# Linear attention on one core: where FP4 weight pieces are unpacked, and in which order the sums around the G products are formed

## The chip, the cores and the metric

The kernel runs on one core of a Trainium2 chip. The metric is the device time of one execution in microseconds (us); a kernel's time is the median of its runs. Less is better. Engine names in this text: PE multiplies matrices, PEld loads its weights, DVE is the vector engine, ACT the activation engine, POOL the general engine, SP issues most DMAs.

## The reference, cut to what matters

Two layers run one after the other on x of 2 x 1024 x 512 (float32), each an attention and an FFN with a residual and a layernorm behind each. Only the first attention and the preparation of the first FFN's weights are touched here:

```
q = elu(x Wq^T) + 1;  k = elu(x Wk^T) + 1;  v = x Wv^T          # 16 heads of 32
kv = k^T v  per head;  z = 1 / (q . sum_t k + 1e-6)
out = (q kv) z;   x = layernorm(x + out Wo^T)
w_gu, w_down = FP4 tables * scales                              # weights of the next FFN
```

The rest (the FFN with these weights, a gated linear attention with chunks of 64, an FFN over the 512 best rows) is computed by code that the change leaves alone.

## The kernel before, in words

The 2048 rows are four blocks of 512 (blk 0 to 3); two blocks make a batch b. The loop `for b in range(B)` (L629 on, in the function `body`) goes through a batch's first attention in the order **k of the first block, k of the second, q of the first, q of the second**. For b = 0 the first k (of block 0) is computed plainly ahead of the loop, so the four passes of seven products that the loop calls k are, in time: k of block 1, then (b = 1) k of blocks 2 and 3; the q passes are those of blocks 0 to 3. "The first k" of the change's title is that of block 1, "the fourth k" that of block 3.

**Seven products instead of eight.** A 512x512 by 512x512 product is cut into a 2x2 of 256-wide parts and done with Winograd's seven products. The price is sums of parts on DVE: S1 = A21 + A22, S2 = S1 - A11, S3 = A11 - A21, S4 = A12 - S2 of the left factor, T1 = B12 - B11, T2 = B22 - T1, T3 = B22 - B12, T4 = B21 - T2 of the right one. `by_seven` (L338) does so for q and k; it is a generator that yields after each of its first products, and `run` (L588) puts a list of other steps into each pause. Its lines in the profile: S1 L356, S2 L357, S3 L358, copies and sums of the results L363 to L384, elu in L304, L305 (ACT) and L306 (DVE).

**From v to G.** `add_xk` (L393, matmuls L400) sums x^T k over a batch. `values` (L452) makes the small per-head matrices from it, `G_rows` (L465) multiplies them with Wo: 32 small matmuls (L473), four ACT copies into G (L477), then the sums T1, T2, T4, T3 of G (`sums_of_weights`, L335, in the order traced). So x + out Wo^T becomes x + q G, with q already weighted by z (`weigh`, L441 to L447).

**The q G products.** `o_products(blk)` (L494) is a generator as well, for blocks 0, 1 and 2; block 3 goes through `add_o` (L542) with whole products. It first forms S1 (L515), S2 (L516) and A21 - A11 in place of A21 (L517), then runs seven products (matmuls at L507); behind each product DVE adds the PSUM bank to x (L513). Products 1, 3, 5 and 7 add up in **one** PSUM bank, grow: product 3 may begin only when L513 has read the sum of product 1, product 7 when L513 has read that of product 5, and product 3 needs S2 and T2. Products 4 and 6 share the bank P7 (side) in the same way, and need A21, T3 and T4. Product 7 needs S4 (L524).

**FP4 pieces.** 27 jobs of `unpack` (L244) turn packed weights into floating point: a DMA of the piece (L248, SP), two passes on DVE (L251, L252), one ACT pass (L254). Pieces of wgu are 128 x 704 (16 of them), then pieces of wdn 128 x 512 (11). Two buffers (`pk`, bufs=2) hold them. The steps `job(n)` in `run` put n jobs into a pause; `unpack_some` ties a job's instructions behind the last elu (L306) that is traced by then.

**What sets the order.** PE's order is written by hand: `behind()` makes each matmul follow the one traced before it. On the other engines the program builder picks, among the instructions that are ready by its own estimate, the one traced first; an engine then works its queue strictly in that order. A tile that takes the place of another of the same tag waits until the last reader of the old one is done. The rooms for G's sums and for S1 are staged[2] in batch 0; in batch 1 they are a tile TG in the place of Wo (tag A3).

Of the kernel before, what the change touches and what calls it, by code (L numbers as in the profile page):

```python
# [10 lines left out]
F32 = mybir.dt.float32  # L11
# [10 lines left out]
P = 128  # L22
# [51 lines left out]
def body(ctx: ExitStack, tc: tile.TileContext, a: dict, out: bass.AP):  # L74
    nc = tc.nc
# [20 lines left out]
    def acc_bank(name):  # L96
        return bank("acc", name)
# [5 lines left out]
    staged = [  # L103
        wfp4.tile([P, to - at, C], F32, tag=f"wdn{i}", name=f"staged{i}")
        for i, (at, to) in enumerate(zip(wdn_parts, wdn_parts[1:]))
    ]
# [20 lines left out]
    def place_w(i, name):  # L127
        return wpool.tile([P, KC, C], F32, tag=f"A{i}", name=name)
# [27 lines left out]
    t, src = new_xT(0)  # L156
# [84 lines left out]
    wk = s1.enter_context(tc.tile_pool(name="s1", bufs=2))  # L241
# [85 lines left out]

    pieces_of = lambda t: t.rearrange("p (k c) -> p k c", k=2)

    def sums_of_weights(w, rooms):  # L330

        B11, B12, B21, B22 = (w[:, 2 * e : 2 * e + 2, 256 * o : 256 * o + 256] for e in range(2) for o in range(2))
        T1, T2, T4, T3 = (*rooms, B12)[:4]
        for dst, x, y in ((T1, B12, B11), (T2, B22, T1), (T4, B21, T2), (T3, B22, B12)):
            nc.vector.tensor_sub(dst, x, y)  # L335
        return T1, T2, T3, T4

    def by_seven(x, w, T, rooms, pairs, ready):  # L338
# [3 lines left out]
        T1, T2, T3, T4 = T  # L342
        S1, S2, S3 = rooms

# [11 lines left out]
        nc.vector.tensor_add(S1, A21, A22)  # L356
        nc.vector.tensor_sub(S2, S1, A11)  # L357
        nc.vector.tensor_sub(S3, A11, A21)  # L358
# [9 lines left out]
        yield  # L368
        product(grow, S2, T2, False)
        nc.scalar.copy(c21, p)  # L370
        side = mm_bank("P7")
        p7 = product(side, S3, T3, True)
        nc.vector.tensor_sub(S2, A12, S2)
        yield
# [4 lines left out]
        yield  # L379
        product(grow, S2, B22, False)  # L380
        elu1(c12, p)
# [8 lines left out]
    pairs_of, mv_of, G_of, acc_of, ksum_of = {}, {}, {}, {}, {}  # L390
# [59 lines left out]
    vkm_of, qT, TG, o_of, parts = {}, {}, {}, {}, []  # L450

    def values(b):  # L452
# [9 lines left out]

        nc.scalar.copy(vkm_of[b], vk.rearrange("p (c d) -> p c d", c=KC))

    def G_rows(b):  # L465


        gp = [acc_bank("gp") for _ in range(4)]
        quad = lambda i: slice(32 * i, 32 * i + 32)
        for j in range(4):  # L470
            for c in range(KC):
                with behind():
                    last_pe[0] = nc.tensor.matmul(  # L473
                        gp[j][quad(c)], vkm_of[b][quad(j), c, quad(j)], Wo[quad(j), c], start=True, stop=True
                    ).ins
        for c in range(KC):
            nc.scalar.copy(G_of[b][:, c], gp[c])  # L477

        room = staged[2] if b == 0 else place_w(3, "TG")
        rooms = slices(room, 0, 3)  # L480
        if b:

            rooms.append(pieces_of(wk.tile([P, 512], F32, tag="qT3", name="T3", bufs=1)))
        TG[b] = sums_of_weights(G_of[b], rooms), pieces_of(room[:, 3])

    def turned(blk, i):
        if i == 0:
# [6 lines left out]
    def o_products(blk):  # L494

        A11, A12, A21, A22 = (qT[blk][:, 2 * e : 2 * e + 2, 256 * t : 256 * t + 256] for t in range(2) for e in range(2))
        G = G_of[blk // 2]
        B11, _, B21, B22 = (G[:, 2 * e : 2 * e + 2, 256 * o : 256 * o + 256] for e in range(2) for o in range(2))
        (T1, T2, T3, T4), S1 = TG[blk // 2]
        S2 = pieces_of(wk.tile([P, 512], F32, tag="qS", name="qS", bufs=1))  # L500

        def product(ps, a, b, first, t, o):

            with behind():
                for r in range(2):
                    for k in range(2):
                        ins = nc.tensor.matmul(  # L507
                            ps[:, 256 * r : 256 * r + 256], a[:, k, r * P : (r + 1) * P], b[:, k],
                            start=first and r == 0 and k == 0, stop=k == 1, skip_group_check=True,
                        ).ins  # L510
            last_pe[0] = ins
            x = x_t[blk][:, 2 * t : 2 * t + 2, 256 * o : 256 * o + 256]
            nc.vector.tensor_add(x, x, ps.rearrange("p (r c) -> p r c", r=2))  # L513

        nc.vector.tensor_add(S1, A21, A22)  # L515
        nc.vector.tensor_sub(S2, S1, A11)  # L516
        nc.vector.tensor_sub(A21, A11, A21)  # L517
        grow = acc_bank("grow")
        product(grow, A11, B11, True, 0, 0)
        yield  # L520
        product(acc_bank("P2"), A12, B21, True, 0, 0)
        yield
        product(grow, S2, T2, False, 1, 0)
        nc.vector.tensor_sub(A12, A12, S2)  # L524
        yield
        side = acc_bank("P7")
        product(side, A21, T3, True, 1, 1)
        yield
        product(grow, S1, T1, False, 1, 1)
        yield  # L530
        product(side, A22, T4, False, 1, 0)
        yield
        product(grow, A12, B22, False, 0, 1)
        yield
        mv = mv_of[blk] = sp.tile([P, 4, 2], F32, tag="mv", name="mv")
        with tc.issue_after(weighed[0]):
            for i in range(4):
                row_stats(mv[:, i], x_t[blk][:, i])
            layernorm(x_t[blk], mv, by=nc.gpsimd)
        yield  # L540
# [57 lines left out]
    def some_xk(blk, *part):  # L598
        return [lambda i=i: add_xk(blk, i) for i in part]

    def turns(blk, *part):
        return [lambda i=i: turned(blk, i) for i in part]

    def some_o(blk, n):

        def one():
            if blk not in o_of:
                o_of[blk] = o_products(blk)
            next(o_of[blk])

        return [one] * n
# [4 lines left out]
    job = lambda n: [lambda: unpack_some(n)]  # L616
# [7 lines left out]
    step = lambda f, *x: [lambda: f(*x)]  # L624
# [4 lines left out]
    for b in range(B):  # L629
        i, j = 2 * b, 2 * b + 1  # L630
        if b:
            run(
                k_products(i),
                turns(1, 0, 1) + job(1), job(1),
                turns(1, 2, 3) + some_o(1, 1) + job(1), some_o(1, 2) + job(1), some_o(1, 5) + job(1),
            )
        q_ready = [] if b else step(q_weights)
        run(
            k_products(j), [],
            some_xk(i, 0, 1) + job(2), some_xk(i, 2) + job(1) + q_ready, some_xk(i, 3) + job(1), job(1 + b),  # L640
        )
        if b == 0:
            Ts["q"] = sums_of_weights(Wq, slices(staged[0], 0, 3))
        else:

            Tq = place_w(1, "Tq")
            for n in range(3):
                nc.scalar.copy(Tq[:, n], staged[0][:, n])
            Ts["q"] = (*slices(Tq, 0, 2), Ts["q"][2], *slices(Tq, 2, 3))
            S_rooms[0] = pieces_of(Tq[:, 3])  # L650
        run(
            q_products(i, lambda t: weigh(i, t)), [],
            some_xk(j, 0, 1) + job(1 + b), some_xk(j, 2) + step(spread_ksum, b) + job(1), some_xk(j, 3) + job(1 + b),
        )
        if b == 0:
            xT[2] = load_xT(2)
        split = [step(split_some, n) if b else [] for n in range(4)]
        rings["free"] = (rings["sum"][(turn_of["sum"] + 1) % 2],)
        run(
            q_products(j, lambda t: None),  # L660
            step(values, b),
            turns(i, 0, 1) + split[0] + job(1 - b),
            turns(i, 2, 3) + split[1] + step(G_rows, b),
            some_o(i, 2) + split[2] + some_o(i, 1) + job(1 - b),
            step(all_free) + some_o(i, 1) + step(weigh, j, 0) + split[3] + some_o(i, 3) + step(weigh, j, 1) + some_o(i, 1)
            + job(1 - b),
        )
        if b == 0:
            xT[3] = load_xT(3)
# [94 lines left out]
    with tc.tile_pool(name="s2", bufs=1) as wk2:  # L764
# [24 lines left out]
        class Chunk:  # L789
# [30 lines left out]
            def step(self, e, k, by):  # L820
                self.product(e, k)
                self.end(e, k, by)

        class Normed:
# [41 lines left out]
            def rest(self):  # L866

                for i in range(4):
                    x = x_t[self.blk][:, i]
                    nc.vector.scalar_tensor_tensor(x, self.y[:, i], self.ms[:, i : i + 1], x, ALU.mult, ALU.add)  # L870
                yield
                for i in range(4):
                    row_stats(self.mv[:, i], x_t[self.blk][:, i])
                layernorm(x_t[self.blk], self.mv)
# [179 lines left out]
    wk = s3.enter_context(tc.tile_pool(name="s3", bufs=1))  # L1054
# [368 lines left out]
    turns, last_hp = [0], [None]  # L1423
# [335 lines left out]
    wk = ctx.enter_context(tc.tile_pool(name="s4", bufs=2))  # L1759
# [4 lines left out]
    room = xT_tile("row")  # L1764
# [78 lines left out]
```

## Time and profile before

| what | us |
|---|---|
| three runs: median (lowest to highest) | 919.6 (917.89 to 919.89) |
| the profiled execution | 917.46 |
| its span, first to last instruction | 915.6 |
| PE busy in the span | 894.0 (98%) |
| DVE busy | 683.3 (75%) |
| ACT, POOL busy | 376.9, 259.3 |
| first attention, about | 0 to 238 of the span |

A page's share of busy time is an average; what a stage is bound by is read from its own stretch. In a row of the timeline the columns are: start in us from the span's beginning, duration in us, engine, line of the kernel, operation, the tiles written and read, shape, the number of instructions put together (x8), and in brackets the idle time of the engine just before and what ended it. The end of a matmul is modelled: eight matmuls of 128x256 are shown with 1.89 or 1.99 us, while the next group starts 1.73 us after them when nothing holds it up; a start that comes later than that is time lost on PE.

### The profile page before, as it was taken

The page shows a single profiled execution, that of the slowest core. Times are in us where ns is not written, and L with a number is a line of the kernel's source. Part 1 is how long each engine was busy: PE and PEld are TensorE (multiplying, and loading weights), DVE is VectorE, ACT ScalarE, POOL GpSimd, SP SyncE. Part 2 cuts the span into 40 slices and gives each one's busy share as a digit, 9 for nine tenths or more (in the row PEclk, how much of TensorE's full clock was granted, in tenths as well). Part 3 has the DMA queues.
Part 4 walks back from the last instruction along what each step waited for, and adds up shares of the span by engine and source line. Part 5 has one row for each costly group of instructions (what it writes and reads, how often), then busy time and mean ns, then how long its engine had stood idle before and what let it go on. Part 6 is the DMA issues. An engine that isn't in the chain of part 4 may idle for free.

```text
span 915.6 us, 10969 instructions
## 1 busy us (share of the span) xinstructions
PE 894.0 (98%) x4037; PEld 699.6 (76%) x4037; DVE 683.3 (75%) x1310; ACT 376.9 (41%) x632; POOL 259.3 (28%) x229
## 2 busy tenths in 40 slices
PE   9999999999999999999998999999999999999996
PEld 6668876687688888888785577788676888888886
DVE  2569994589777787787777866766977886898535
ACT  2345343453476877877874424130301223120000
POOL 1120074200663456655663301010160030000012
PEclk9999999999999999999999999999999999999999
DMA  9622221100300001001003300000024220230001
GB/s 325 217 90 78 78 70 47 58 1 0 127 1 1 1 0 47 1 1 47 1 1 128 126 1 1 0 1 1 1 93 137 92 70 24 94 137 0 13 35 47
DMA packets 26135, 50.17 MB, mean 55 GB/s; under 512 B 4798, under 2 KB 5482, under 8 KB 25569
## 3 DMA queue, kind: packets, MB, share of 16 engines
q1 hardware_dynamic: 23441, 44.34, 14.3%
q0 software_dynamic: 1920, 4.22, 1.2%
q10 hardware_dynamic: 720, 0.92, 0.4%
q8 instruction: 32, 0.52, 0.2%
q14 instruction: 22, 0.18, 0.1%
HBM read 41.03 MB, written 10.54 MB: 56 GB/s over the span
## 4 chain that ended last, share of the span: by engine, by line
PE 77%; DVE 14%; ACT 3%; issue 2%; POOL 2%; DMA 1%; SPq 0%; POOLq 0%; ACTq 0%; DVEq 0%
PE yp L1527 10%; PE hp L1443 9%; PE yp L783 9%; PE gatep L783 8%; PE upp L783 8%; PE go L1198 6%; PE xk L400 6%; PE grow L349 4%; PE P L349 3%; PE ao L547 2%; PE ao L1316 2%; PE grow L1282 1%; PE kp L573 1%; DVE cmp L1367 1%; DVE cmp L1364 1%
## 5 line engine op out<-in xcount | busy, mean ns | idle before, releaser
L843 DVE TENSOR_TENSOR yp<-yp,ratio 128x512 f32<-128x512 f32 x160 | 103.3, 693 | 9.7 <-PE yp L783 9.5
L201 POOL TENSOR_TENSOR rs<-rs,table 128x4 f32<-128x4 f32 (+1 forms) x20 | 18.2, 912 | 302.3 <-DVE rs L200 302.1
L809 ACT ACTIVATE gatep<-gatep,scale 128x512 f32<-128x512 f32 x132 | 85.0, 656 | 35.0 <-PE gatep L783 32.2
L783 PE MATMUL yp<-wdn,hhi 128*128 128x512 f32 x176 | 71.2, 405 | 0.0
L783 PE MATMUL yp<-wdn,hlo 128*128 128x512 f32 x176 | 70.0, 397 | 1.0 <-POOL hlo L818 1.0
L783 PE MATMUL gatep<-x1Th,wgu 128*128 128x512 f32 x176 | 70.3, 399 | 0.0
L783 PE MATMUL gatep<-x1Tl,wgu 128*128 128x512 f32 x176 | 69.2, 393 | 0.3 <-DVE x1Tl L232 0.3
L783 PE MATMUL upp<-x1Tl,wgu 128*128 128x512 f32 x176 | 69.0, 392 | 0.0
L783 PE MATMUL upp<-x1Th,wgu 128*128 128x512 f32 x176 | 68.8, 391 | 0.0
L809 ACT ACTIVATE upp<-upp,scale 128x512 f32<-128x512 f32 x82 | 54.3, 662 | 12.0 <-PE upp L783 8.0
L818 POOL TENSOR_TENSOR hlo<-whole,hhi 128x512 fp32r<-128x512 f32 x43 | 55.7, 1296 | 3.5
L817 POOL CAST hhi<-whole 128x512 fp32r<-128x512 f32 x43 | 26.4, 613 | 99.6 <-DVE whole L815 98.5
L815 DVE SCALAR_TENSOR_TENSOR whole<-upp,scale,silu 128x512 f32<-128x512 f32 x43 | 32.3, 751 | 27.2 <-PE upp L783 21.2
L811 DVE TENSOR_SCALAR upp<-upp,scale 128x512 f32<-128x512 f32 x50 | 37.5, 752 | 9.5 <-PE upp L783 8.3
L1198 PE MATMUL go<-big 128*128 128x256 f32 x192 | 43.9, 381 | 0.0
L208 DVE BATCH_NORM_STATS2 st<-x 128x6 f32<-128x512 f32 x64 | 42.4, 677 | 0.4
L400 PE MATMUL xk<-pair,x 128*128 128x512 f32 x96 | 42.7, 592 | 0.0
L1198 PEld LDWEIGHTS go<-big 128*128 128x128 f32 x192 | 35.9, 190 | 6.3 <-DVE q L1105 0.8
L783 PEld LDWEIGHTS gatep<-x1Th,wgu 128*128 128x128 f32 x176 | 33.1, 188 | 9.7 <-ACT gatep L809 1.2
L783 PEld LDWEIGHTS yp<-wdn,hlo 128*128 128x128 f32 x176 | 33.1, 188 | 8.7 <-POOL hlo L818 1.7
L783 PEld LDWEIGHTS gatep<-x1Tl,wgu 128*128 128x128 f32 x176 | 33.1, 188 | 8.1 <-DVE x1Tl L232 0.6
L783 PEld LDWEIGHTS upp<-x1Th,wgu 128*128 128x128 f32 x176 | 33.1, 188 | 7.4 <-DVE rw L815 0.2
(454 smaller groups left out, 2091.6 us busy)
## 6 DMA issues: line engine op xcount, KB each, us to landing
pk<-in_gu SPq DMA_DIRECT2D x16, 352.0 KB, 3.6
x<-in_x SPq DMA_DIRECT2D x4, 1024.0 KB, 14.9
w<-in_w SPq DMA_DIRECT2D x1, 4096.0 KB, 12.1
xs<-picked SPq DMA_DIRECT2D x4, 1024.0 KB, 5.0
out<-x SPq DMA_DIRECT2D x4, 1024.0 KB, 4.2
w<-in_w SPq DMA_DIRECT2D x4, 1024.0 KB, 6.5
x0T<-in_xT SPq DMA_DIRECT2D x3, 1024.0 KB, 7.1
pk<-in_dn SPq DMA_DIRECT2D x11, 256.0 KB, 3.1
```

The costliest lines, as they stand in the source:

```text
L208: nc.vector.bn_stats(st, x)
L349: ins = nc.tensor.matmul(ps[:, 256 * r : 256 * r + 256], a[:, k, r * P : (r + 1) * P], b[:, k], start=first and r == 0 and k == 0, stop=k ...
L400: ins = nc.tensor.matmul(acc_of[b][c], x_t[blk][:, i, c * P : (c + 1) * P], pairs_of["k", blk][i // 2][:, i % 2], start=blk % 2 == 0 and i ...
L783: nc.tensor.matmul(ps, w, x, start=start and n == 0, stop=stop and n == 1, skip_group_check=True)
L809: nc.scalar.activation(ps, ps, AF.Copy, scale=s)
L811: nc.vector.tensor_scalar(ps, ps, s, None, ALU.mult)
L815: nc.vector.scalar_tensor_tensor(self.whole, ps, s, self.silu, ALU.mult, ALU.mult)
L818: nc.gpsimd.tensor_sub(lo, self.whole, hi.bitcast(F32))
L843: nc.vector.tensor_tensor(self.y[:, i] if g == NI - 1 else ps, ps, ratio[:, g], ALU.mult)
L1198: ins = nc.tensor.matmul(ps[:, 256 * m : 256 * m + 256], w[:, k, m], b[:, k, 256 * half : 256 * half + 256], start=first and m == 0 and k ...
L1443: ins = nc.tensor.matmul(ps[:, 256 * j : 256 * j + 256], w[:, k, 2 * g + j], x[:, k], start=k == 0, stop=k == 1).ins
L1527: nc.tensor.matmul(ps[:, 256 * r : 256 * r + 256], x(r, j), w(j), start=j == 0, stop=j == NJ - 1)
```

## The change

Three things move; no arithmetic is added or dropped.

1. **Pieces.** The number of FP4 jobs by pass, before and after: k of block 1: 5, 6; q of block 0: 3, 4; q of block 1: 3, 1; k of block 2: 5, 2 (all at its end); k of block 3: 6, 9; q of block 2: 5, 5. The total of 27 and their order are the same.
2. **q's first sums.** For the first block of a batch S1 and S2 (L515, L516) are traced by a new `q_sums`, called just ahead of `G_rows` instead of in `o_products`.
3. **Two of G's sums, and A21.** `G_rows` forms T1 and T2 only; T4 and T3 are traced in `o_products` behind product 1 with its addition to x, and so is A21 - A11.

```diff
-    def sums_of_weights(w, rooms):
+    def sums_of_weights(w, rooms, part=range(4)):
...
-        for dst, x, y in ((T1, B12, B11), (T2, B22, T1), (T4, B21, T2), (T3, B22, B12)):
-            nc.vector.tensor_sub(dst, x, y)
+        steps = (T1, B12, B11), (T2, B22, T1), (T4, B21, T2), (T3, B22, B12)
+        for i in part:
+            nc.vector.tensor_sub(*steps[i])
...
+    def TG_room(b):
+        if b not in TG_rooms:
+            TG_rooms[b] = staged[2] if b == 0 else place_w(3, "TG")
+        return TG_rooms[b]
+
+    TG_rooms, TG_rest, S_of = {}, [], {}
+
+    def q_sums(blk):
+
+        A11, A12, A21, A22 = (qT[blk][:, 2 * e : 2 * e + 2, 256 * t : 256 * t + 256] for t in range(2) for e in range(2))
+        S1 = pieces_of(TG_room(blk // 2)[:, 3])
+        S2 = pieces_of(wk.tile([P, 512], F32, tag="qS", name="qS", bufs=1))
+        nc.vector.tensor_add(S1, A21, A22)
+        nc.vector.tensor_sub(S2, S1, A11)
+        S_of[blk] = S1, S2
...
-        room = staged[2] if b == 0 else place_w(3, "TG")
+        room = TG_room(b)
...
-        TG[b] = sums_of_weights(G_of[b], rooms), pieces_of(room[:, 3])
+        TG[b] = sums_of_weights(G_of[b], rooms, range(2))
+        TG_rest.append(lambda: sums_of_weights(G_of[b], rooms, range(2, 4)))
...
-        nc.vector.tensor_add(S1, A21, A22)
-        nc.vector.tensor_sub(S2, S1, A11)
-        nc.vector.tensor_sub(A21, A11, A21)
+        if blk not in S_of:
+            q_sums(blk)
+        S1, S2 = S_of[blk]
         grow = acc_bank("grow")
         product(grow, A11, B11, True, 0, 0)
+        for rest in TG_rest:
+            rest()
+        TG_rest.clear()
+        nc.vector.tensor_sub(A21, A11, A21)
...
                 k_products(i),
-                turns(1, 0, 1) + job(1), job(1),
-                turns(1, 2, 3) + some_o(1, 1) + job(1), some_o(1, 2) + job(1), some_o(1, 5) + job(1),
+                turns(1, 0, 1), [],
+                turns(1, 2, 3) + some_o(1, 1), some_o(1, 2), some_o(1, 5) + job(2),
...
             k_products(j), [],
-            some_xk(i, 0, 1) + job(2), some_xk(i, 2) + job(1) + q_ready, some_xk(i, 3) + job(1), job(1 + b),
+            some_xk(i, 0, 1) + job(2 + b), some_xk(i, 2) + job(1 + b) + q_ready, some_xk(i, 3) + job(2), job(1 + b),
...
             q_products(i, lambda t: weigh(i, t)), [],
-            some_xk(j, 0, 1) + job(1 + b), some_xk(j, 2) + step(spread_ksum, b) + job(1), some_xk(j, 3) + job(1 + b),
+            some_xk(j, 0, 1) + job(2), some_xk(j, 2) + step(spread_ksum, b) + job(1), some_xk(j, 3) + job(1 + b),
...
             step(values, b),
-            turns(i, 0, 1) + split[0] + job(1 - b),
-            turns(i, 2, 3) + split[1] + step(G_rows, b),
-            some_o(i, 2) + split[2] + some_o(i, 1) + job(1 - b),
+            turns(i, 0, 1) + split[0],
+            turns(i, 2, 3) + split[1] + step(q_sums, i) + step(G_rows, b),
+            some_o(i, 2) + split[2] + some_o(i, 1),
```

More of the change, by code (lines that the diff above doesn't have):

```diff
@@ L498, in o_products @@
         B11, _, B21, B22 = (G[:, 2 * e : 2 * e + 2, 256 * o : 256 * o + 256] for e in range(2) for o in range(2))
-        (T1, T2, T3, T4), S1 = TG[blk // 2]
-        S2 = pieces_of(wk.tile([P, 512], F32, tag="qS", name="qS", bufs=1))
+        T1, T2, T3, T4 = TG[blk // 2]
         def product(ps, a, b, first, t, o):
```

## The prediction

> **What bounds the kernel now.** I read the page first, then busy time by stretches of 20 us, then the timeline of PE and DVE around the products that the diff touches. The page says that PE ends the work:
>
> ```profile
> PE 894.0 (98%) x4037; PEld 699.6 (76%) x4037; DVE 683.3 (75%) x1310; ACT 376.9 (41%) x632; POOL 259.3 (28%) x229
> PE 77%; DVE 14%; ACT 3%; issue 2%; POOL 2%; DMA 1%; SPq 0%; POOLq 0%; ACTq 0%; DVEq 0%
> ```
>
> So a microsecond counts only where PE stands still. The stretches (time of the stretch, then PE, PEld, DVE, ACT, POOL busy) show where in the first attention that is:
>
> ```profile
> 80.00:100.00 20.00, 19.29 (x117) 15.48 (x116) 18.64 (x35) 11.15 (x20) 0.00 (x0) 1.00 0.17 47
> 100.00:120.00 20.00, 18.85 (x93) 15.73 (x91) 19.82 (x45) 6.73 (x12) 4.76 (x2) 1.00 0.23 79
> 120.00:140.00 20.00, 18.97 (x80) 15.07 (x81) 18.95 (x32) 7.74 (x13) 13.97 (x9) 1.00 0.20 64
> 140.00:160.00 20.00, 20.00 (x70) 12.91 (x69) 9.53 (x16) 7.33 (x14) 10.46 (x5) 1.00 0.17 52
> 200.00:220.00 20.00, 18.71 (x106) 15.37 (x87) 16.69 (x31) 7.72 (x15) 0.00 (x0) 1.00 0.00 1
> ```
>
> PE loses time where DVE is full (18.6 to 19.8 of 20, from 80 to 140), none in the fourth k and third q (140 to 200), and some again at 200. In PE's timeline the losses are all at q G products (L507), each behind a DVE instruction:
>
> ```profile
> 92.12 1.99 PE L507 MATMUL grow<-staged,qS 128*128 128x256 f32 x8 [0.71 <-DVE x L513]
> 103.83 1.99 PE L507 MATMUL grow<-G,staged 128*128 128x256 f32 x8 [0.68 <-DVE x L513]
> 120.21 1.99 PE L507 MATMUL grow<-staged,qS 128*128 128x256 f32 x8 [0.55 <-DVE qS L516]
> 131.66 1.56 PE L507 MATMUL grow<-G,staged 128*128 128x256 f32 x6 [0.82 <-DVE x L513]
> 207.47 1.99 PE L507 MATMUL grow<-TG,qS 128*128 128x256 f32 x8 [0.98 <-DVE x L513]
> ```
>
> Their price by starts: eight such matmuls pass in 1.73 us. Product 2 of block 0 starts at 89.52, so product 3 could start at 91.25; it starts at 92.12 (0.87 lost), and the first pair after a wait takes 0.10 more (1.99 against 1.89), together 0.97. Likewise: product 6 of block 0 at 101.16 0.40, its product 7 at 103.83 0.94, product 3 of block 1 at 120.21 0.82, its product 7 at 131.66 1.08, product 3 of block 2 at 207.47 (after product 2 at 204.16 and four transposes of 0.43) 1.25. That is 5.46 us in all, the most that these places can give.
>
> **Part by part.** Durations are the rows'; DVE's step from one start to the next is 0.60 for a 128x512 sum, 0.49 for L251, 0.43 for L252.
>
> *Block 0, product 3.* DVE's queue ahead of it:
>
> ```profile
> 83.97 0.58 DVE L251 TENSOR_SCALAR pk<-pk,shift 128x704 int32<-128x704 int32 x1
> 85.07 0.52 DVE L252 TENSOR_SCALAR pk<-pk 128x704 int32<-128x704 int32 x1
> 85.50 0.68 DVE L515 TENSOR_TENSOR staged<-staged 128x512 f32<-128x512 f32 x1
> ...
> 91.39 0.68 DVE L513 TENSOR_TENSOR x<-x,grow 128x512 f32<-128x512 f32 x1
> ```
>
> S1 and S2 already run ahead of the sums of G here, although the code traces them later: the builder fills gaps. So their move is worth nothing in batch 0, and the same gap-filling may keep T3, T4 and A21 ahead of L513 whatever the code says. What counts is the piece that goes. DVE loses 0.49 + 0.43 of queue, but T2 (L335 at 88.38, 0.26 of idle before it) waits for G's copies on ACT, which began at 86.31, behind the piece's ACT pass (85.62, 0.79). Without that pass they can begin once the small matmuls are through, between 85.5 and 86.0; T2 is then 0.3 to 0.8 earlier. With the four instructions between T2 and L513 unchanged, product 3 gains 0.3 to 0.8; with T3 and T4 behind L513 (2 x 0.60 less) it gains all of 0.97. I take 0.85. Cover gone: if the builder adds A21 and T's in front, 0.3.
>
> *Block 1, product 3.* It waits for S2. Four passes of two pieces stand between 110.21 and S2 in DVE's unbroken queue (0.41, 0.40, 0.51, 0.43 by starts: 1.75). All go, as k of block 2 keeps pieces only at its end. S2 needs 0.82 less: all 0.82 is gained, with 0.93 to spare. S1 cannot start before ACT's qT copy ends at 116.35, 1.7 before it does now, so this leaves the result. DVE and PE enter this stretch together (L513 at 105.86 waits for PE), so what block 0 gains is kept.
>
> *Block 1, product 7.*
>
> ```profile
> 129.26 1.75 DVE L306 SCALAR_TENSOR_TENSOR pair<-pair,e 128x512 f32<-128x512 f32 x1
> 130.93 0.68 DVE L513 TENSOR_TENSOR x<-x,grow 128x512 f32<-128x512 f32 x1
> ```
>
> Two more pieces (0.94 + 0.72 + 0.50 + 0.44 = 2.6 by starts) go from 120.68 to 126.86, so DVE has caught up here and meets PE. For it: L306 comes earlier. Against it: L306 takes 1.75 here and 0.69 elsewhere, beside POOL's k sums (L419, 128.69, 1.77), which move along; and the two pieces left at the end of k of block 2 may now fill the gap ahead of L513 (beside POOL one such pass takes 1.27 or 1.47, at 131.53 and 132.84). From 0 (or a loss of 0.5) to 1.08; I take half, 0.55.
>
> The Trainium skill, "SBUF — State Buffer", section "Who interferes with whom", holds that DVE with two SBUF inputs, or in a 2-port mode, and POOL exclude each other for a whole instruction. L306 agrees: L419 ends at 130.46, and 0.6 later is 131.06 against 131.01. S1 at 118.03 does not: it ends at 119.12, inside a POOL pass (L203) that lasts until 120.02. By the rule each of the six passes moved into the fourth k could wait for a whole L203 of some 2.6 us, an estimate of up to 15.6 us of DVE there; by the rows it is at most some 1 us each.
>
> *Block 0, products 6 and 7 (1.34).* They wait for L513 behind the weighing of block 1 (L441 to L447), whose order is unchanged; at 95.88 and 97.17 DVE itself waits for PE and ACT, so fewer pieces do not help. I take 0, bounds 0 to 1.34.
>
> *Block 2, product 3.* No piece runs here. S1 lies in the place of Wo, so it can't run before the small matmuls of `G_rows` (199.31 to 200.6) have read Wo: ahead of G's copies, yes, ahead of G's matmuls, no. DVE idles 0.77 before T1 and 0.29 before the next sum, waiting for ACT's copies:
>
> ```profile
> 201.54 0.69 DVE L335 TENSOR_TENSOR TG<-G 128x512 f32<-128x512 f32 x1 [0.77 <-ACT G L477]
> 202.52 0.69 DVE L335 TENSOR_TENSOR T<-G 128x512 f32<-128x512 f32 x1 [0.29 <-ACT G L477]
> ...
> 206.74 0.68 DVE L513 TENSOR_TENSOR x<-x,grow 128x512 f32<-128x512 f32 x1
> ```
>
> S1 (0.60) fits into the first gap and S2 or A21 partly into the second: L513 0.9 earlier with nothing else reordered, enough for all 1.25 where T3, T4 or A21 go behind it. I take 1.0, bounds 0 and 1.25.
>
> *What is added.* One piece each in k of block 1 and q of block 0: DVE idles 3.91 before 65.17 and 2.42 before 38.49, PE loses nothing from 22 to 84; cost 0, and without that cover 0.9 each. SP's queue: the loads of x^T (L147) stand behind piece loads (0.54 each); that at 72.05 is first used at 90.79 and lands in some 7 us, so 11 us cover it. Three pieces more in the fourth k: 3 x 0.92 of DVE against 10.5 idle in 140 to 160; cost 0, and the first rival if not. T3, T4 and A21 are needed first at product 4 (97.41 in block 0, 212.75 in block 2), over 5 us later: 0.
>
> **Sum:** 0.85 + 0.82 + 0.55 + 1.0 = 3.2 us. PE's order is fixed and it is full from 140 to 200 and again from 220, so the gain carries to the end. The profiled execution took 917.46 (span 915.6 and 1.86 around it): it becomes 914.3. Three runs have a median of 919.6, 2.1 above that, between 917.89 and 919.89; against the median I forecast **916.4**.
>
> **Rivals.**
> - *The fourth k runs dry (slower).* A buffer's cycle is 0.54 issue + 3.5 to landing + 0.92 DVE + 0.63 ACT, 5.6 us; with two buffers 2.8 a piece, 25 us for nine, and the pass is 25.8 us long (133.49 to 159.31). DVE works in order, so it stands when a piece is late. It does so now:
>
> ```profile
> 146.36 0.49 DVE L251 TENSOR_SCALAR pk<-pk,shift 128x512 int32<-128x512 int32 x1 [3.06 <-DMA pk<-in_dn]
> ```
>
>   If each of three pieces costs such a stall, 9.2 us; the nearest deadline is k's part at 159.45 for the x^T k products at 162.76, 2.6 us of slack. Past that PE stops: 9.2 - 2.6 - 3.2 = +3.4, **923.0**. Against it: that stall of 3.06 cost PE nothing, and six pieces fit with half of DVE idle. It decides from 2.6 us of stall just ahead of L306.
> - *The order eats it (within 0.2%).* The builder keeps T3, T4 and A21 ahead of L513 and POOL keeps L306 slow: 0.3 + 0.82 + 0 + 0.4 = 1.5, **918.1**. For it: L356 of the next pass ran ahead of L513 at 90.79, so the builder thinks PE later than it is.
> - *All of it.* Products 6 and 7 of block 0 start on time too: 5.4, **914.2**. Against it: the weighing ahead of them is not moved.
> - *A wash.* Half the stalls of the first rival eat the gain: **919.6**.
>
> **Chances.** Forecast (gain 2.2 to 4.4) 0.50; order eats it 0.20; all of it 0.10; a wash 0.08; fourth k dry 0.12. A measurement of this kernel can tell about 0.2% (1.8 us) from no change: faster 0.50 + 0.10 + 0.04 of the second case = 0.64; within 0.16 + 0.08 = 0.24; slower 0.12. The range takes in all but the slower case and the upper half of the wash: 913.8 to 919.6, with the runs' own spread of some 1 us either way inside it.
>
> **What would show it.** Right: in the profile after, no idle time before product 3 of blocks 0, 1 and 2; pieces absent between 83 and 97 and from 110 to 129; PE without gaps in 140 to 200; L515 before the first L335 in batch 1 as well. Wrong: L251 rows with idle for a DMA in the fourth k followed by idle PE at L400, or L335 and L517 still ahead of L513 with the same 0.7 to 1.0 of idle PE.

## The result and the profile after

The changed kernel takes **921.28 us** (median of 20 runs, 918.61 to 923.03) against 919.16 of the kernel before (20 runs, 917.46 to 922.31): ratio **1.0022**, 95% interval 1.0013 to 1.0031. It is slower by some 2 us, where 3.2 us of gain were forecast. The profiled execution has a span of 920.2 us against 915.6. Lines of the kernel have moved: the seven products of k and q are at L350, the q G products at L524, their additions to x at L530, q's first sums at L478 and L479, A21 - A11 at L540, the copy of c21, one quarter of a product's result, at L371 (L370 before), the pieces still at L251, L252 and L254.

The stretches of the changed kernel (length, then PE, PEld, DVE, ACT and POOL busy) answer to those shown of before:

```profile
60.00:80.00 20.00, 18.61 (x83) 12.78 (x83) 14.59 (x28) 9.68 (x16) 0.00 (x0) 1.00 0.48 144
80.00:100.00 20.00, 19.99 (x125) 16.15 (x124) 17.73 (x33) 9.60 (x17) 0.00 (x0) 1.00 0.00 1
120.00:140.00 20.00, 19.08 (x85) 15.75 (x84) 17.60 (x29) 6.50 (x10) 14.68 (x9) 1.00 0.12 36
160.00:180.00 20.00, 18.98 (x62) 11.34 (x61) 12.43 (x20) 8.89 (x16) 5.24 (x4) 1.00 0.25 79
180.00:200.00 20.00, 18.42 (x99) 15.28 (x100) 16.28 (x35) 10.77 (x20) 0.00 (x0) 1.00 0.04 14
200.00:220.00 20.00, 20.00 (x129) 16.62 (x128) 16.73 (x31) 10.80 (x19) 0.00 (x0) 1.00 0.00 1
```

In the kernel before, PE was full in three of them:

```profile
60.00:80.00 20.00, 20.00 (x98) 15.03 (x97) 14.11 (x28) 9.48 (x17) 0.00 (x0) 1.00 0.31 100
160.00:180.00 20.00, 20.00 (x67) 12.35 (x66) 11.07 (x19) 7.82 (x14) 5.25 (x4) 1.00 0.20 66
180.00:200.00 20.00, 20.00 (x139) 16.59 (x141) 17.13 (x36) 11.80 (x21) 0.00 (x0) 1.00 0.00 1
```

PE no longer stands at 80 to 100 and at 200 to 220, where gains were forecast. It now stands at 60 to 80 and around 180, where it never stood before. PE's timeline of the changed kernel names who holds it up; the bracket is the idle time and its end:

```profile
65.59 1.99 PE L350 MATMUL grow<-staged,Tk 128*128 128x256 f32 x8 [1.31 <-ACT pair L371]
94.23 1.99 PE L524 MATMUL grow<-staged,qS 128*128 128x256 f32 x8
121.60 1.89 PE L524 MATMUL grow<-staged,qS 128*128 128x256 f32 x8
133.04 1.99 PE L524 MATMUL grow<-G,staged 128*128 128x256 f32 x8 [0.92 <-DVE x L530]
171.07 1.89 PE L350 MATMUL grow<-Tq,rw 128*128 128x256 f32 x8
181.58 1.99 PE L350 MATMUL grow<-Tq 128*128 128x256 f32 x8 [2.60 <-ACT pair L371]
210.63 1.89 PE L524 MATMUL grow<-TG,qS 128*128 128x256 f32 x8
```

Product 3 of blocks 1 and 2 starts with no wait (121.60 and 210.63), that of block 0 (94.23) is 0.18 late. The two new waits are not at a q G product at all: they are in `by_seven`, in the q passes of blocks 0 and 2, and the engine waited for is ACT. The product S1 T1 adds into the bank grow, and may begin only when ACT has copied c21 out of it (L371). ACT's timeline of the changed kernel shows what stands ahead of that copy:

```profile
58.14 0.79 ACT L254 ACTIVATE wgu<-pk 128x704 fp32r<-128x704 f16 x1 [1.95 <-DVE pk L252]
61.26 0.79 ACT L254 ACTIVATE wgu<-pk 128x704 fp32r<-128x704 f16 x1 [2.34 <-DVE pk L252]
64.27 0.79 ACT L254 ACTIVATE wgu<-pk 128x704 fp32r<-128x704 f16 x1 [2.22 <-DVE pk L252]
64.97 0.57 ACT L371 COPY pair<-grow 128x512 f32<-128x512 f32 x1
...
176.57 0.63 ACT L254 ACTIVATE wdn<-pk 128x512 fp32r<-128x512 f16 x1 [0.43 <-DVE pk L252]
180.42 0.63 ACT L254 ACTIVATE wdn<-pk 128x512 fp32r<-128x512 f16 x1 [3.22 <-DVE pk L252]
180.96 0.57 ACT L371 COPY pair<-grow 128x512 f32<-128x512 f32 x1
```

In the kernel before, the same queue had one piece fewer ahead of the copy (PE's rows are the products that use the bank next):

```profile
60.09 0.79 ACT L254 ACTIVATE wgu<-pk 128x704 fp32r<-128x704 f16 x1 [2.19 <-DVE pk L252]
60.78 0.57 ACT L370 COPY pair<-grow 128x512 f32<-128x512 f32 x1
63.24 1.89 PE L349 MATMUL grow<-staged,Tk 128*128 128x256 f32 x8
...
172.75 0.63 ACT L254 ACTIVATE wdn<-pk 128x512 fp32r<-128x512 f16 x1 [0.58 <-DVE pk L252]
173.29 0.57 ACT L370 COPY pair<-grow 128x512 f32<-128x512 f32 x1
177.04 0.63 ACT L254 ACTIVATE wdn<-pk 128x512 fp32r<-128x512 f16 x1 [3.19 <-DVE pk L252]
177.38 1.89 PE L349 MATMUL grow<-Tq 128*128 128x256 f32 x8
```

Read them as queues. What the copy needs was ready long before (the product S2 T2 starts at 171.07 in the changed kernel and passes in some 1.9 us), but ACT works in order, and the piece ahead of the copy waits for DVE's pass, which waits for a load. The timelines of DVE and of the DMA issues (SPq) of the changed kernel show that last step:

```profile
58.95 0.54 SPq L248 DMA_DIRECT2D pk<-in_gu  x1
63.09 0.58 DVE L251 TENSOR_SCALAR pk<-pk,shift 128x704 int32<-128x704 int32 x1 [1.86 <-DMA pk<-in_gu]
65.09 0.54 SPq L248 DMA_DIRECT2D pk<-in_gu  x1
...
179.44 0.48 DVE L251 TENSOR_SCALAR pk<-pk,shift 128x512 int32<-128x512 int32 x1 [2.90 <-DMA pk<-in_dn]
```

The load is late because of its buffer: it is issued at 58.95, just as the ACT pass of the piece two before (58.14, 0.79) ends, DVE starts on the piece at 63.09, its own ACT pass ends at 65.06, and the next load into this buffer is issued at 65.09. That is 6.1 us round, with two buffers one piece of 128x704 in 3.1 us, however idle DVE and ACT are. For a 128x512 piece in block 2's q pass the same round, from issue to issue, is 4.9 us (176.16 to 181.08).

**The sum by starts.** Two matmuls that both kernels have in the same order of work stand for the stretch, the first row of each pair from before, the second from the changed kernel:

```profile
57.22 1.89 PE L349 MATMUL P<-Wq,b 128*128 128x256 f32 x8
58.10 1.89 PE L350 MATMUL P<-Wq,b 128*128 128x256 f32 x8
...
218.37 0.24 PE L679 MATMUL pg<-table,sg 88*128 88x88 f32 x1
221.43 0.24 PE L700 MATMUL pg<-table,sg 88*128 88x88 f32 x1
```

Between them lie 161.15 us before and 163.33 after: +2.18, of which the places named in this document, priced as in the prediction, make 2.12. The medians differ by 2.12 too. That the two agree so closely is luck: a profile is one execution, and the runs of the changed kernel lie between 918.61 and 923.03. Of the rest of the span's 4.6, 0.9 is a first load of x^T that came later in this execution (its second group of matmuls starts at 8.10 instead of 7.22), and another 1.6 fell at a half clock at 532 to 536 (last section).

### The profile page after: what moved, and what is told of

Read it like the earlier page. It is cut to its first block, busy times and chain, and to the rows that moved or that the text cites. A ratio compares the mean times of both kernels' runs of the same rounds, so it can differ in the third digit from the quotient of the medians.

```text
span 920.2 us, 10974 instructions
## 1 busy us (share of the span) xinstructions
PE 896.5 (97%) x4037; PEld 700.9 (76%) x4037; DVE 684.0 (74%) x1310; ACT 377.0 (41%) x632; POOL 257.2 (28%) x229
## 4 chain that ended last, share of the span: by engine, by line
PE 73%; DVE 14%; ACT 4%; DMA 4%; issue 2%; POOL 2%; SPq 0%; POOLq 0%; DVEq 0%; ACTq 0%
PE yp L1548 10%; PE hp L1464 9%; PE yp L804 9%; PE gatep L804 8%; PE upp L804 8%; PE go L1219 6%; PE grow L350 3%; PE P L350 2%; DMA pk<-in_gu 2%; PE grow L524 2%; PE ao L568 1%; PE ao L1337 1%; PE xk L401 1%; DVE pk L251 1%; PE grow L1303 1%
```

## The experiments

"Lost" is the time between these two matmuls in the kernel's profile, one execution each, less the 161.15 of before. "Ahead" is how many of the 27 ACT passes stand ahead of the copy of c21, in ACT's instruction order, in the q passes of blocks 0 and 2. Ratios are to runs of the kernel before on the same chip.

| kernel | ahead | lost, us | ratio (95% interval) |
|---|---|---|---|
| before | 7, 24 | 0 | 1 |
| the change | 8, 25 | +2.18 | 1.0022 (1.0013 to 1.0031) |
| sums_only | 7, 24 | -1.23 | 0.9985 (0.9972 to 0.9998) |
| pieces_only | 8, 25 | +3.12 | 1.0042 (1.0023 to 1.0061) |
| q0_three | 8, 25 | +1.44 | 1.0019 (1.0006 to 1.0032) |
| late_as_before | 8, 24 | -0.28 | 0.9996 (0.9984 to 1.0008) |
| early_as_before | 7, 25 | +2.84 | 1.0032 (1.0020 to 1.0044) |
| three_buffers | 9, 25 | -2.66 | 0.9967 (0.9954 to 0.9980) |
| pinned | 7, 24 | -0.03 | 1.0015 (1.0005 to 1.0024) |
| pinned_more | 7, 24 | -0.09 | 1.0005 (0.9991 to 1.0019) |
| before_three | 7, 25 | +0.03 | 0.9999 (0.9985 to 1.0013) |
| three_more | 9, 25 | -3.83 | 0.9952 (0.9935 to 0.9968) |
| q_ahead | 7, 24 | -0.96 | 0.9989 (0.9976 to 1.0002) |
| T_later | 7, 24 | -1.23 | 0.9988 (0.9976 to 0.9999) |

A thousandth is 0.92 us.

### Which half of the change loses

sums_only is the changed kernel with every `job(...)` as in the kernel before; pieces_only is the kernel before with the changed kernel's `job(...)`.

> The new order of the sums with every FP4 piece in the pass that it had in the kernel before. My theory: the loss comes from the pieces, by the activation engine's queue, where one more piece stands ahead of the copy of c21 that TensorE waits for in the q passes of blocks 0 and 2 (1.47 + 0.10 + 0.25 + 0.10 and 2.76 + 0.10 us of lost TensorE time in the profile of the changed kernel). Then this kernel has neither of these waits and keeps the gain at product 3 of block 2 (1.25): 919.2 - 1.25 = 917.9 us, ratio 0.9986. Rival, the new order of the sums itself puts the program's later work out of step: 921 us or more, with the wait of some 2.8 us in the q pass of block 2.

> The pieces moved as in the change, the sums as in the kernel before. My theory: both new waits are there (+1.92 and +2.86), the gains at product 3 of blocks 0 and 1 too (-0.70 and -0.82), product 7 of block 1 +0.10, nothing at block 2: +3.4, 922.5 us, ratio 1.0037. Rival, the sums make the loss: 917.6 to 919.2, ratio at most 1.000.

Measured: 917.12 (ratio 0.9985) and 922.11 (1.0042), both as the theory had it. In the profile of pieces_only PE loses 1.19 and 0.45 in block 0's q pass and 2.56 in block 2's; sums_only loses nothing in either, and nothing at product 3 of block 2. The rival is out: the pieces lose, and the sums gain (by an interval that ends just under 1, 0.9998, and by the wait that is gone from the profile).

### Which pieces

```diff
 q0_three:
-            some_xk(j, 0, 1) + job(2), some_xk(j, 2) + ...
+            some_xk(j, 0, 1) + job(1 + b), some_xk(j, 2) + ...
...
-            + job(1 - b),
+            + job(2 - 2 * b),
```

> The changed kernel, but the q pass of block 0 keeps its three pieces (the fourth goes to the end of the q pass of block 1). My theory: the wait for the copy of c21 in the q pass of block 0 goes (1.9), that of block 2 stays (2.9): 921.3 - 1.9 = 919.4 us, ratio to before 1.0002. Rival, it is the sixth piece in the k pass of block 1 that pushes the copy back: no change, 921.3.

> The changed kernel, but k of blocks 2 and 3 have five and six pieces at the places that they had before; the q pass of block 2 has its five in both. My theory: the wait of 2.86 in the q pass of block 2 comes from the pieces that reach it later, so it goes; product 3 of block 1 waits again (+0.82 or less), the wait of block 0 stays: 921.3 - 2.9 + 0.7 = 919.1 us, ratio 1.0000. Rival, the wait in block 2's q pass comes from the order of the sums or from the earlier passes: 921.5 to 922.

> The changed kernel, but the first batch's pieces where they were before (5 in k of block 1, 3 in q of block 0, 3 in q of block 1), the second batch as changed. In the activation engine's queue 7 pieces then stand ahead of the copy of c21 in block 0's q pass, as in the kernel before, instead of 8. My theory: that wait (1.92 in all) goes, product 3 of block 0 waits again (+0.70), the wait in block 2's q pass stays at 1.8 to 2.8: 2.1 - 1.9 + 0.7 = +0.9 us, ratio 1.001. Rival, the wait in block 2's q pass depends on where the first batch's pieces are: it goes as well, ratio 0.998.

q0_three came out at 919.85 (1.0019), not at 1.0002: a miss, and its rival holds: the sixth piece in k of block 1 is enough. Taking the fourth piece out of block 0's q pass did not change how many stand ahead of the copy (8), since the sixth piece of the pass before still does, and the wait for the copy stayed (1.17 against 1.47). At two buffers the sum of all pieces up to that point counts, not those of one pass. late_as_before (918.50, 0.9996) and early_as_before (920.98, 1.0032) separate the two batches: with 24 ahead the wait in block 2's q pass is absent, with 7 ahead that of block 0's. early_as_before was expected at 1.0010 and is slower. In its profiled execution the wait of 2.86 was followed by matmuls at half speed (last section), another 1.6 us; whether this happened in its other five runs no profile shows.

### Is it the number ahead, or that their loads are late?

three_buffers gives the pieces a third buffer:

```diff
-    dq = s1.enter_context(tc.tile_pool(name="dq", bufs=2))
+    dq = s1.enter_context(tc.tile_pool(name="dq", bufs=3))
...
-        s = wk.tile([n, 2, P], F32, name="dn_scale", bufs=1)
-        r = wk.tile([n, P], F32, name="dn_ratio", bufs=1)
+        room = wk.tile([P, 512], F32, tag="qT3", name="dn_room", bufs=1)
+        s = room[:n, :256].rearrange("p (i c) -> p i c", i=2)
+        r = room[:n, 256:384]
```

> The changed kernel with a third buffer for packed pieces; to make room, two small rooms of the scales' preparation share another tile. The builder now puts 9 pieces ahead of the copy of c21 in block 0's q pass and 25 in block 2's. My theory: the piece is late because its load has to wait for a buffer that is freed only two pieces earlier; with three, loads run ahead, and both waits of TensorE fall below 0.3 although still more pieces stand ahead: 2.1 - 1.6 - 2.6 = -2.1 us, ratio 0.998. Rival, the number of pieces ahead of the copy is what counts and their loads don't: no better than the changed kernel, ratio 1.002 or more.

Measured: 914.85 (0.9967), faster than both kernels. ACT's timeline of three_buffers in block 2's q pass:

```profile
170.68 1.82 ACT L254 ACTIVATE wdn<-pk 128x512 fp32r<-128x512 f16 x3 [2.63 <-DVE pk L252]
172.41 0.57 ACT L372 COPY pair<-grow 128x512 f32<-128x512 f32 x1
```

As many pieces stand ahead of the copy as in the changed kernel (three directly ahead, 25 in all), but they run one after the other, and the copy is done at 172.98, long before PE wants it (176.01). So the number ahead is harmless by itself: with two buffers the pieces are late. Of the 3.1 us gained, the lost time has 2.66; the rest is open. before_three, the same buffer in the kernel before, shows that it is worth nothing where no piece is in PE's way:

> The kernel before with nothing changed but a third buffer for packed pieces (two small rooms of the scales' preparation share another tile to make room). My theory: the third buffer helps the changed kernel by 5 us only because its pieces hold TensorE up; in the kernel before no wait of TensorE is due to a piece, so ratio 1.000, between 0.999 and 1.001. Rival, a third buffer is worth 3 us by itself, whatever the pieces' places: 0.997.

Measured: 918.30, 0.9999 (0.9985 to 1.0013). The builder put 25 pieces ahead of the copy in block 2's q pass here too, and PE did not wait there: with three buffers, once more, the number does no harm.

### Can the copy be put ahead instead?

pinned keeps two buffers and ties each ACT pass behind the copy of c21 traced last; pinned_more and three_more also tie a piece's passes on DVE behind the addition of a q G product.

```diff
 pinned:
-        nc.scalar.activation(dst, half, AF.Copy, scale=UNIT)
+        with ExitStack() if c21_copy[0] is None else tc.issue_after(c21_copy[0]):
+            nc.scalar.activation(dst, half, AF.Copy, scale=UNIT)
...
-        nc.scalar.copy(c21, p)
+        c21_copy[0] = nc.scalar.copy(c21, p).ins
...
-            some_xk(j, 0, 1) + job(2), some_xk(j, 2) + step(spread_ksum, b) + job(1), some_xk(j, 3) + job(1 + b),
+            some_xk(j, 0, 1) + job(1 + b), some_xk(j, 2) + step(spread_ksum, b) + job(2 - b), some_xk(j, 3) + job(1 + b),
 pinned_more, and three_more on three_buffers:
-            nc.vector.tensor_add(x, x, ps.rearrange("p (r c) -> p r c", r=2))
+            anchor[0] = nc.vector.tensor_add(x, x, ps.rearrange("p (r c) -> p r c", r=2)).ins
```

> The changed kernel, two buffers; a piece's pass on the activation engine is tied behind the last copy of c21 traced by then, and one piece of block 0's q pass is traced one pause later. So 7 and 24 pieces stand ahead of the copy, as in the kernel before, and each pass keeps its number of pieces. My theory: the waits for the copy go in both q passes, all gains stay: 2.1 - 1.6 - 2.8 = -2.3 us, ratio 0.9975. Rival, DVE's own standing for late pieces holds TensorE up by another way: ratio 1.000 or more.

> As the kernel with the tied passes, and besides a piece's passes on DVE are tied behind the last addition of a q G product to x as well as behind the last elu. My theory: the two pieces at the end of k of block 2 no longer run ahead of the addition of product 5 of block 1, so its product 7 does not wait (1.19 us in the changed kernel): -2.3 - 1.1 = -3.4 us, ratio 0.9963. Rival, POOL beside elu's sum (1.75 us instead of 0.69) holds that addition up, as in the kernel before: no better than without it, 0.9975.

Neither gained: 919.72 (1.0015) and 918.17 (1.0005). In the profile of pinned the waits for the copy are indeed gone, but another took their place:

```profile
75.67 2.50 PE L462 MATMUL vk<-G,Wv 128*128 128x128 f32 x20 [1.84 <-DVE pair L387]
```

L387 is the last sum of c21, one step behind an elu whose ACT half (L306 in this kernel) waits behind the last piece of the pass: ACT's pass of the piece, L255 at 72.36, waits 1.34 for DVE, and L306 follows at 73.05. The load of this piece is not what is late: DVE's pass on it (71.18) shows no wait for a DMA, it runs right behind the elu of 70.57 that it is tied to. So putting one instruction of PE's chain ahead of the pieces leaves the next one behind them. The rival to my expectation had the number, and that TensorE would be held up by another way; the way was ACT's queue, not DVE standing for a late piece. pinned's loss by starts is the same as before's (-0.03), yet its ratio is 1.0015. In its profile, which is its slowest execution (921.18), TensorE is at half clock between 500 and 510 and at 530 to 535, and between 207 and 541 it falls 3.7 us further behind the kernel before, all of it around these two places; its five fastest runs, with a mean clock of 0.997 to 0.999, took 917.29 to 918.31. So I put the rest down to the clock, though no run here separates it. pinned_more loses no time at product 7 of block 1, but 0.58 and 0.39 at 157 and 165 instead, in the fourth k and third q, and 1.9 ahead of L462 like pinned.

> The changed kernel with three buffers, and a piece's passes on DVE tied behind the last addition of a q G product to x. My theory: the wait of 1.19 us at product 7 of block 1 goes as it did with two buffers, and the waits that came in its place there (0.58 and 0.39 in the fourth k and third q) don't, since loads run ahead: -3.1 - 1.1 = -4.2 us, ratio 0.9954. Rival, the tied pieces come late here too and the gain is given back: 0.9967 as without the tie.

Measured: 914.70 (0.9952): with loads in time the tie costs nothing, and the wait at product 7 of block 1 is gone from its profile. Its interval overlaps that of three_buffers, so the runs alone don't settle that it is the faster of the two; the lost time does point that way (-3.83 against -2.66).

### Which order of the sums gains

```diff
 q_ahead, on sums_only:
-        TG[b] = sums_of_weights(G_of[b], rooms, range(2))
-        TG_rest.append(lambda: sums_of_weights(G_of[b], rooms, range(2, 4)))
+        TG[b] = sums_of_weights(G_of[b], rooms)
...
+        nc.vector.tensor_sub(A21, A11, A21)
         grow = acc_bank("grow")
...
-        nc.vector.tensor_sub(A21, A11, A21)
 T_later, on sums_only:
-            turns(i, 2, 3) + split[1] + step(q_sums, i) + step(G_rows, b),
+            turns(i, 2, 3) + split[1] + step(G_rows, b),
```

> The kernel before with only one of the new orders: S1 and S2 of q traced ahead of G's copies; the four sums of G and A21 - A11 stay where they were, and so do all pieces. My theory: DVE's idle time before T1 and the next sum (0.77 and 0.29) takes up S1 and part of S2, so the addition behind product 1 of block 2 comes 1.0 earlier and product 3 gains 1.0 of its 1.25: ratio 0.9989. Rival, this half does nothing alone and the later T3 does it all: 1.000.

> The kernel before with only the other new order: T3, T4 and A21 - A11 traced behind product 1 with its addition; S1 and S2 and all pieces as before. My theory: the builder puts T3 and A21 of block 2 behind that addition, which comes 1.2 earlier: product 3 gains all of its 1.25, nothing in batch 0, where gaps are filled as before: ratio 0.9986. Rival, only both together work: 1.000.

Measured: 917.42 (0.9989) and 917.23 (0.9988). Either half alone removes the wait at product 3 of block 2 nearly or wholly (lost -0.96 and -1.23); both together (sums_only, -1.23) remove no more, since there is no more there. q_ahead's interval just reaches 1.

## Why the prediction was wrong, point by point

**The step that failed** is "What is added", with its two zeros: "One piece each in k of block 1 and q of block 0: ... cost 0" and "Three pieces more in the fourth k: ... cost 0". They cost 1.92 (1.47 + 0.10 at the copy, 0.25 + 0.10 at the next wait, of the matmuls vk at 76.28) and 2.86 (2.76 + 0.10). I asked only whether DVE had idle time to cover the passes. It had; but a piece passes through three queues, and the one that hurt was ACT's, where the pass L254 stands in order ahead of a copy that PE waits for. In the profile of before the slack of that copy could be read: L370 ends at 61.35 and PE uses the bank at 63.24, 1.9 us; in block 2's q pass 3.5 (173.86 to 177.38). So could the price of one more piece ahead of it: at 3.1 us a piece the one behind 60.09 would be through at about 64, an estimate, and the piece that in before follows the copy of block 2 ends its ACT pass at 177.67. Both are behind PE's use. In block 2 the wait is longer than that one piece makes it, since the pass's first two pieces also come 2.5 us later, measured against S2 T2 (DVE starts on them at 167.22, 3.85 ahead of it; before at 163.32, 6.31 ahead).

**The first rival had the cause, in the wrong place.** It named the two buffers and their cycle (5.6 us reckoned; 4.9 measured for a piece of 128x512, 6.1 for one of 128x704) and gave the slower side a chance of 0.12. But it looked for the harm in the fourth k, at elu on DVE, where the pieces were added. There PE loses nothing (140 to 160 is full); DVE stands there, 4.16 at 148.96, and PE does not wait. The harm came in the next pass, which has the same five pieces as before: they start later there, and the builder put one more of them ahead of the copy.

**Gains, by the same steps.** Block 0, product 3: 0.85 forecast, 0.69 found, and it comes from the piece that went (pieces_only has it, sums_only has not); T3, T4 and A21 stayed ahead of the addition, as the prediction feared. Block 1, product 3: 0.82 and 0.82. Block 2, product 3: 1.0 and 1.25. Block 1, product 7: 0.55 forecast, a loss of 0.10 found: the first DVE pass of both pieces left at the end of k of block 2 ran ahead of the addition, as the DVE rows of the changed kernel show (the second of the two starts at 130.81 and takes 1.58):

```profile
129.92 2.48 DVE L251 TENSOR_SCALAR pk<-pk,shift 128x704 int32<-128x704 int32 x2
132.32 0.67 DVE L530 TENSOR_TENSOR x<-x,grow 128x512 f32<-128x512 f32 x1
```

three_more, where these pieces are tied behind, loses nothing at this product. Products 6 and 7 of block 0: 0 and 0. Together 2.66 of gain where 3.2 was forecast, so the gains were nearly right; with the two costs, 2.66 - 1.92 - 2.86 = -2.12.

**POOL.** Beside its layernorm in the fourth k DVE's first passes (L251) on the pieces took 0.75 to 0.89 each instead of 0.5 (142.02, two in 1.51; 148.96, 0.89). The price of a whole POOL instruction for each, by the rule of the Trainium skill, "SBUF — State Buffer", section "Who interferes with whom", is not seen there.

## What to carry to other kernels

Before moving work into idle time, follow every queue that it passes through, not only the engine that looks full: list what stands behind it, in order, on each engine, and read the slack of each instruction there that the bounding engine waits for. A piece that comes through a small ring of buffers has a rate of its own (here 3.1 us for 128x704 at two buffers, however idle DVE and ACT are), and it is the sum of pieces up to a point, not the number within a pass, that makes the next one late. Where such a rate is the limit, one more buffer (0.9967 with the changed order, 0.9999 without) did here what reordering could not.

## What the runs showed of the hardware

**The clock after a wait.** In early_as_before the wait for the copy was 0.10 longer than in the changed kernel (2.86 against 2.76 by starts), and TensorE then ran at half speed. Its PE timeline, and its stretches, where the number behind the busy times is the granted clock:

```profile
179.93 3.59 PE L350 MATMUL grow<-Tq 128*128 128x256 f32 x8 [2.70 <-ACT pair L371]
```

```profile
176.00:179.90 3.90, 1.24 (x3) 0.19 (x1) 2.07 (x4) 1.12 (x3) 0.00 (x0) 1.00 0.37 125
179.90:181.00 1.10, 1.07 (x3) 0.89 (x4) 0.04 (x1) 0.47 (x1) 0.00 (x0) 0.62 0.27 47
181.00:182.00 1.00, 1.00 (x3) 0.77 (x3) 0.00 (x0) 0.00 (x0) 0.00 (x0) 0.50 0.57 211
182.00:183.00 1.00, 1.00 (x4) 0.78 (x3) 0.00 (x0) 0.00 (x0) 0.00 (x0) 0.50 0.00 0
183.00:184.00 1.00, 1.00 (x4) 0.67 (x3) 0.44 (x1) 0.44 (x1) 0.00 (x0) 0.71 0.00 0
184.00:186.00 2.00, 2.00 (x6) 0.83 (x5) 1.54 (x3) 1.18 (x4) 0.00 (x0) 1.00 0.04 8
```

Eight matmuls took 3.59 instead of 1.99, and the clock was whole again at 184. The changed kernel shows the same at 532 to 536 (clock 0.54 and 0.61), behind a wait of 1.78 on PE that follows other short ones: it is 3.01 us behind the kernel before at 530.71 and 4.65 behind at 541.42, another 1.6. The profile of before has a wait of 1.77 at the same place (527.70) and a clock of 1.00 behind it. So half clock followed waits of 1.78 and 2.86, and none followed waits of 1.77 and 2.76: it comes in some executions and not in others, and the length of the one wait does not decide. That the waits bring it on is argued from the order in time; no run here tests it. The runs of one kernel spread by some 5 us (before, 917.2 to 922.7), with a mean clock from 0.999 down to 0.993. The change may have cost time by this way as well: 11 of its 20 runs have a mean clock below 0.997, of the kernel before 9 of the 83 runs taken beside the experiments.

The Trainium skill, "TensorE: Matmul & The Clock Gate", section "Part 1: The HAM clock gate", gives half clock after at least one idle window of about 3.4 us, in windows that run freely. If the clock is either whole or half, the stretches above give half clock for 0.84 + 1.00 + 1.00 + 0.58 = 3.4 us; this and the chance from run to run agree with the page. The length of the idle time does not: half clock began behind a wait of 2.86 us here.
